# Splitting the first loads over two queues and shortening the run of filler products at the start of an AdaLN-FFN kernel

## The chip, the cores and the metric

One Trainium2 chip, one core of it. The metric is the device time of one execution in microseconds, median of several runs. TensorE (PE) does the matrix products, VectorE (DVE), ScalarE (ACT) and GpSimd (POOL) the elementwise work, and SyncE (SP) and ACT issue the DMAs that this text speaks of.

## The reference, cut to what matters

`x` is 64 x 64 x 512 in f32 (batch, row, feature) and `cond_1024` is 64 x 256. The first part of the computation is the one that the change touches:

```python
q_emb = relu(cond @ W3 + b3)                 # 64 x 512, "the condition"
v_sum = sum(v, axis=1, keepdims=True)        # over the 64 rows of a batch
x = (n * v + v_sum) * q_emb[:, None, :]      # "modulation", n = 64
y = relu(x @ W2 + b2)
```

The second part is an FFN on `y`: a base product with `W_base`, a shared low-rank product, six low-rank experts that are weighted by the two largest of six softmax gates, and their sum with the input.

## The kernel before

The features lie on the 128 partitions (512 = 4 chunks `c`), the 4096 rows along the free axis, in 4 blocks `k` of 1024 rows (16 batches of 64). Block 0 is done by `first_mixed`, blocks 1 to 3 by `first_inner`, and behind each comes the FFN. From the second half of block 0 on, the products use schemes with seven instead of eight partial products, whose operand sums DVE makes (`t2`, `inner_t`, `s`). The order on each engine is the order in which the program issues the instructions.

**The start.** SP issues the loads one after the other:

- `head_sb`, 196 KB: the condition, the two biases (136 columns of f32 in all, `NH0`) and the first quarter of W3 (256 columns);
- `xa` number 0, 128 KB: the first 4 batches of chunk 0; then `w2` chunk 0, 256 KB; `xa` number 1, the next 4 batches; `w3`, 384 KB, the other three quarters of W3; then `x0` and `w2` for the other chunks, in turn; the FFN's weights; and block 1 of `x`.

The DMAs of SP and ACT use eight completion semaphores in turn, so that a load is issued only when the one eight places ahead of it has landed.

On ACT a one-column activation (line 108) comes first, and with it the load of the activation table. On PE, `first_mixed` begins with `idle(8)`: eight bf16 products of a constant tile of ones, 128 x 512, whose output is not used. Then comes `embed([0], ...)`, the condition's product for the first 128 features: four matmuls (an f32 product is two matmuls here), which read `head_sb`, and an ACT Relu into `q_sb`. Then `idle(2)`. Then for each chunk `c`:

- `modulate_group` on DVE: the batch sums (line 245), `n * v + v_sum` (line 255, two instructions) and the product with `q_sb` (line 259);
- the products `py` (line 409) with the four output blocks `f` of `w2` chunk `c`. Chunk 0 is done in two pieces of 4 batches, eight matmuls each, and behind the first piece comes `embed(range(1, NC))`, twelve matmuls that need `w3`;
- `modulate_scalar` for the other eight batches of the chunk before: sums and two small products on DVE, then eight ACT instructions (line 267).

When the four chunks are done, DVE makes the sums `t`, `inner_t` and `s` (lines 141 to 154 and 280 to 283), of which the product at line 181 that follows is the first reader.

Of the kernel before, what the change touches and what calls it, by code (L numbers as in the profile page):

```python
# [16 lines left out]
P = 128  # L17
# [10 lines left out]
DH = D // 2  # L28
# [10 lines left out]
def adaln_ffn(ctx: ExitStack, tc: tile.TileContext, xa, x0, x1, head, w3, w2, wb, a, bcat, bb, br, outT):  # L39
# [8 lines left out]
    nc = tc.nc  # L48
# [12 lines left out]
    def temps(name):  # L61

        return {n: tmp.tile([P, KH, TB], F32, tag=n, name=f"{n}_{name}") for n in pair_tags}

    def load_x(k):
        xs[k] = xpool.tile([P, NC, 2, TB], F32, tag="x", name=f"x_{k}")
        for c in CHUNKS:
            nc.sync.dma_start(xs[k][:, c].rearrange("p h t -> p (h t)"), x1[k, c])
# [18 lines left out]
    NH0 = NQ * B + 2 * NC  # L87
    head_sb = const.tile([P, NH0 + NQ * P], F32, tag="head_sb", name="head_sb")
# [4 lines left out]
    w2_sb = const.tile([P, NC, D], F32, tag="w2_sb", name="w2_sb")  # L93
# [7 lines left out]
    def load_xa(n):  # L101
        nc.sync.dma_start(xs[0][:, 0, ts(n, TB // 2)], xa[n])

    def load_w2(c):
        nc.sync.dma_start(w2_sb[:, c, :], w2[ts(c, P), :])

    nc.sync.dma_start(head_sb, head)
    nc.scalar.activation(scratch, ones[:, :1], AF.Relu)
    load_xa(0)
    load_w2(0)  # L110
    load_xa(1)
    nc.sync.dma_start(w3_sb, w3)
    for c in range(1, NC):
# [75 lines left out]
    def idle(n):  # L189
        p = ps_p.tile([P, TB], F32, tag="pp", name="idle")  # L190
        for _ in range(n):
            nc.tensor.matmul(p, ones[:, :P], ones, start=True, stop=True)

    def embed(fs, name):
        pq = ps_h.tile([P, len(fs), B], F32, tag="ph", name=name)
        for n, f in enumerate(fs):
            for c in range(NQ):
                nc.tensor.matmul(
                    pq[:, n], w3_of[f][:, c], cond_sb[:, c, :], start=(c == 0), stop=(c == NQ - 1)
                )  # L200
        for n, f in enumerate(fs):
            nc.scalar.activation(q_sb[:, f, :], pq[:, n], AF.Relu, bias=b3_sb[:, f : f + 1])
# [44 lines left out]
    def modulate_group(v, vsum, c, lo, hi):  # L247

        nb = hi - lo
        batch_sums(vsum, c, lo, hi)  # L250
        xc = batches_of(c, lo, hi)
        vc = v[:, c, :, lo * NH : hi * NH].rearrange("p h (b n) -> p h b n", n=NH)
        sc = vsum[:, c, lo:hi]
        for h in range(2):
            nc.vector.scalar_tensor_tensor(
                vc[:, h], xc[:, h], float(N), sc.unsqueeze(2).to_broadcast([P, nb, NH]), ALU.mult, ALU.add
            )
        q = q_sb[:, c, lo:hi].unsqueeze(1).unsqueeze(3).to_broadcast([P, 2, nb, NH])
        nc.vector.tensor_tensor(vc, vc, q, ALU.mult)

    def modulate_scalar(v, vsum, nq, c, lo, hi):

        batch_sums(vsum, c, lo, hi)
        nc.vector.tensor_scalar(nq[:, c, lo:hi], q_sb[:, c, lo:hi], float(N), None, ALU.mult)
        nc.vector.tensor_tensor(vsum[:, c, lo:hi], vsum[:, c, lo:hi], q_sb[:, c, lo:hi], ALU.mult)  # L265
        for b in range(lo, hi):
            nc.scalar.activation(  # L267
                v[:, c, :, ts(b, NH)], batches_of(c, b, b + 1)[:, :, 0], AF.Identity,
                bias=vsum[:, c, b : b + 1], scale=nq[:, c, b : b + 1],
            )  # L270

    def row_sums(a, name, cols=slice(0, TB)):

        all_s = mid.tile([P, 4, KH, TB], F32, tag=name, name=name)
        s = [all_s[:, i, :, cols] for i in range(4)]
        a11, a12, a21, a22 = a[:, :KH, 0, cols], a[:, KH:, 0, cols], a[:, :KH, 1, cols], a[:, KH:, 1, cols]

        def steps(c=slice(0, KH), fourth=nc.vector):
            return [
                lambda: nc.vector.tensor_tensor(s[0][:, c], a21[:, c], a22[:, c], ALU.add),  # L280
                lambda: nc.vector.tensor_tensor(s[1][:, c], s[0][:, c], a11[:, c], ALU.subtract),
                lambda: nc.vector.tensor_tensor(s[2][:, c], a11[:, c], a21[:, c], ALU.subtract),
                lambda: fourth.tensor_tensor(s[3][:, c], a12[:, c], s[1][:, c], ALU.subtract),
            ]

        return {1: a11, 2: a12, 3: s[3], 4: a22, 5: s[0], 6: s[1], 7: s[2], "sums": all_s}, steps
# [6 lines left out]
    def fill(n):  # L293
        for _ in range(min(n, len(behind))):
            for step in behind.pop(0):
                step()
# [100 lines left out]
    def first_mixed(y):  # L397

        vs[0] = v = xpool.tile([P, NC, 2, TB], F32, tag="x", name="v_0")
        vsum = small.tile([P, NC, BB], F32, tag="vsum", name="vsum_0")
        nq = small.tile([P, NC, BB], F32, tag="nq", name="nq_0")
        half, cols = BB // 2, BB // 2 * NH
        other = slice(cols, TB)
        s, s_steps = row_sums(v, "s", other)

        def part(p, c, f, lo, hi):
            nc.tensor.matmul(  # L409
                p[:, :, lo * NH : hi * NH], w2_sb[:, c, ts(f, P)], v[:, c, :, lo * NH : hi * NH],  # L410
                start=(c == 0 and lo == 0), stop=(c == NC - 1), skip_group_check=True,
            )

        def without_sums(c):
            for j in range(KH):
                nc.tensor.matmul(
                    px[:, j], w2_sb[:, c, ts(j, P)], v[:, c, 0, other],
                    start=(c == 0 and j == 0), stop=(c % KH == KH - 1),
                    skip_group_check=True,
                )  # L420

        idle(8)
        embed([0], "pq0")
        idle(2)
        p0 = [ps_p.tile([P, 2, cols], F32, tag="pp", name=f"py_{f}") for f in range(NC)]

        px = ps_p.tile([P, KH, cols], F32, tag="pp", name="yx_0")
        p1 = mid.tile([P, 4, 1, R2], F32, tag="inner_s1", name="p1_0").rearrange("p n o t -> p (n o t)")
        p1 = p1[:, : KH * cols].rearrange("p (j t) -> p j t", j=KH)
        for c in range(NC):  # L430
            pieces = ((0, half // 2), (half // 2, half)) if c == 0 else ((0, half),)
            for lo, hi in pieces:
                modulate_group(v, vsum, c, lo, hi)
                for f in range(NC):
                    part(p0[f], c, f, lo, hi)
                if c == 0 and lo == 0:
                    embed(range(1, NC), "pq")
            if c > 0:
                modulate_scalar(v, vsum, nq, c - 1, half, BB)
            if c == KH:  # L440
                for n in range(KH):
                    without_sums(n)
        nc.scalar.copy(p1, px)
        modulate_scalar(v, vsum, nq, NC - 1, half, BB)
        for f in range(NC):
            nc.scalar.activation(y[:, f, :, :cols], p0[f], AF.Relu, bias=b2_sb[:, f : f + 1])
        for c in range(KH, NC):
            without_sums(c)
        load_x(2)
        for step in t2_steps + inner_steps[:4] + s_steps():  # L450
            step()
        prepare(1, tb_steps + inner_steps[4:])
        fill(1)
        pairs = temps(0)
        for j in range(KH):
            relu(y, j, 0, px[:, j], other)
        banks = [ps_p.tile([P, KH, cols], F32, tag="pp", name=f"y{n}_0") for n in "ywz"]
        for j in range(KH):
            f1, f2 = j, KH + j
            temp = lambda n: pairs[n][:, j, :cols]  # L460
            py, pw, pz = (p[:, j] for p in banks)
            u, r, r1, r2 = temp("u"), temp("u22"), temp("u21"), temp("u12")
            product(py, 6, j, t2, s, start=j == 0)
            nc.vector.tensor_tensor(u, py, p1[:, j], ALU.add)
            product(pw, 5, j, t2, s, start=j == 0)
            nc.vector.tensor_tensor(r, pw, u, ALU.add)
            product(pz, 7, j, t2, s, start=j == 0)
            nc.vector.tensor_tensor(r, pz, r, ALU.add)  # L468
            relu(y, f2, 1, r, other)
            fill(1)  # L470
            product(pw, 3, j, t2, s, start=False)
            nc.vector.tensor_tensor(r2, pw, u, ALU.add)
            relu(y, f2, 0, r2, other)
            fill(1)
            product(pz, 4, j, t2, s, start=False)
            nc.vector.tensor_tensor(r1, pz, u, ALU.add)
            relu(y, f1, 1, r1, other)
            fill(1)
# [921 lines left out]
```

## Time and profile before

| | |
|---|---|
| median of 3 runs | 253.53 us (253.40 to 253.58) |
| the profiled execution | 253.81 us, span 252.0 us |
| PE busy | 246.8 us, 98% of the span |
| DVE, ACT, POOL busy | 203.8, 158.0, 126.2 us |
| DMA | 33.82 MB, mean 134 GB/s |

The span runs from the first to the last profiled instruction of the program; 1.81 us of the profiled execution's time lie outside it. Times in the profile are us from the start of the span. In a row of the timeline stand the start, the time from the first start to the last end, engine, line, operation, output<-inputs, shapes, the number of instructions, and in brackets how long the engine had been idle and what released it. Names are given without their numbers: `w_sb` stands for `w2_sb` and `w3_sb`, `pq` for both of the condition's products. A matmul's printed duration is longer than its share of PE, since matmuls overlap; the distance between starts is what one costs.

### The profile page before, as it was taken

The page shows a single profiled execution, that of the slowest core. Times are in us where ns is not written, and L with a number is a line of the kernel's source. Part 1 is how long each engine was busy: PE and PEld are TensorE (multiplying, and loading weights), DVE is VectorE, ACT ScalarE, POOL GpSimd, SP SyncE. Part 2 cuts the span into 40 slices and gives each one's busy share as a digit, 9 for nine tenths or more (in the row PEclk, how much of TensorE's full clock was granted, in tenths as well). Part 3 has the DMA queues.
Part 4 walks back from the last instruction along what each step waited for, and adds up shares of the span by engine and source line. Part 5 has one row for each costly group of instructions (what it writes and reads, how often), then busy time and mean ns, then how long its engine had stood idle before and what let it go on. Part 6 is the DMA issues. An engine that isn't in the chain of part 4 may idle for free.

```text
span 252.0 us, 3678 instructions
## 1 busy us (share of the span) xinstructions
PE 246.8 (98%) x1134; PEld 189.4 (75%) x1134; DVE 203.8 (81%) x407; ACT 158.0 (63%) x436; POOL 126.2 (50%) x150
## 2 busy tenths in 40 slices
PE   8999999999999999999999999999999999999993
PEld 3846897454468889857888889947888889966783
DVE  2899998879996988999995778999992576797472
ACT  2299588579018889797638889796826428252310
POOL 1000000009707579059469968339659894059850
PEclk9999999999999999999999999999999999999999
DMA  6997818000431024835459922306259852500054
GB/s 181 370 350 274 330 28 307 0 3 16 151 125 42 3 86 138 336 147 216 61 80 195 156 94 101 127 25 250 28 79 197 138 133 97 166 1 0 9 194 134
DMA packets 17482, 33.82 MB, mean 134 GB/s; under 512 B 1605, under 2 KB 3781, under 8 KB 17462
## 3 DMA queue, kind: packets, MB, share of 16 engines
q1 hardware_dynamic: 13910, 27.09, 30.3%
q0 software_dynamic: 3264, 6.29, 15.9%
q10 hardware_dynamic: 288, 0.20, 0.3%
q8 instruction: 9, 0.15, 0.2%
q14 instruction: 11, 0.09, 0.1%
HBM read 19.94 MB, written 14.68 MB: 137 GB/s over the span
## 4 chain that ended last, share of the span: by engine, by line
PE 96%; DMA 2%; DVE 0%; SPq 0%; issue 0%
PE ia L502 14%; PE ph L1337 11%; PE ib L502 11%; PE ha L987 10%; PE hb L987 8%; PE oz L181 7%; PE py L409 6%; PE oy L181 6%; PE ja L987 4%; PE jb L987 3%; PE ox L181 3%; PE ow L181 3%; DMA w_sb<-in_w_dram 2%; PE yw L181 1%; PE pt L649 1%; PE yz L181 1%
## 5 line engine op out<-in xcount | busy, mean ns | idle before, releaser
L229 ACT ACTIVATE x<-x,vsum,nq 128x64 f32<-128x64 f32 x176 | 63.3, 431 | 1.4 <-DVE vsum L221 1.4
L656 POOL TENSOR_TENSOR hwd<-hwT 113x512 f32<-113x512 f32 x4 | 5.1, 1271 | 55.4 <-ACT hwT L651 55.4
L1337 PEld LDWEIGHTS ph<-a_sb,y 128*128 128x128 f32 x256 | 30.7, 192 | 0.8
L1337 PE MATMUL ph<-a_sb,y 128*128 128x118 f32 x256 | 30.7, 275 | 0.0
L493 DVE TENSOR_TENSOR u<-ib,u 128x256 f32<-128x256 f32 x42 | 16.4, 418 | 11.9 <-PE ib L502 11.8
L493 DVE TENSOR_TENSOR u<-ia,u 128x256 f32<-128x256 f32 (+1 forms) x36 | 16.1, 462 | 7.1 <-ACT u L540 5.8
L508 ACT COPY ib<-ia 128x256 f32<-128x256 f32 x21 | 7.6, 361 | 17.2 <-PE ia L502 17.2
L395 ACT ACTIVATE y<-u,head_sb 128x256 f32<-128x256 f32 (+1 forms) x30 | 15.8, 583 | 3.7 <-DVE u L468 3.0
L502 PE MATMUL ib<-inner_s,inner_t 128*128 128x256 f32 x60 | 17.4, 379 | 0.0
L219 DVE TENSOR_REDUCE vsum<-x 128x8 f32<-128x512 f32 x24 | 15.5, 676 | 0.0
L181 PE MATMUL oz<-sy,tb 128*128 128x512 f32 x32 | 15.0, 592 | 0.0
L409 PE MATMUL py<-v,w_sb 128*128 128x512 f32 (+1 forms) x40 | 14.4, 510 | 0.6 <-DMA w_sb<-in_w_dram 0.6
L181 PE MATMUL oy<-sy,tb 128*128 128x512 f32 x32 | 14.7, 597 | 0.0
L511 ACT COPY ib<-ib 128x256 f32<-128x256 f32 x21 | 7.6, 360 | 9.0 <-PE ib L502 8.6
L502 PEld LDWEIGHTS ib<-inner_s,inner_t 128*128 128x128 f32 x60 | 11.4, 190 | 1.6
L409 PEld LDWEIGHTS py<-v,w_sb 128*128 128x128 f32 x40 | 7.4, 190 | 6.7 <-issue 4.8
L344 POOL TENSOR_TENSOR sy<-sy 128x256 f32<-128x256 f32 x4 | 3.8, 952 | 17.2 <-PE oy L181 17.2
L267 ACT ACTIVATE v<-x,vsum,nq 128x64 f32<-128x64 f32 x32 | 11.0, 429 | 1.7 <-DVE vsum L265 1.7
L744 POOL DMA_DIRECT2D out_dram<-y x8 | 10.8, 1688 | 0.7 <-ACT ib L508 0.7
L181 PEld LDWEIGHTS oy<-sy,tb 128*128 128x128 f32 x32 | 5.8, 190 | 6.8 <-issue 6.2
L502 PE MATMUL ia<-s,t 128*128 128x256 f32 x36 | 10.2, 379 | 0.0
L181 PEld LDWEIGHTS oz<-sy,tb 128*128 128x128 f32 x32 | 5.8, 190 | 5.8 <-issue 5.3
(321 smaller groups left out, 679.9 us busy)
## 6 DMA issues: line engine op xcount, KB each, us to landing
xu<-in_x_dram SPq DMA_DIRECT2D x14, 512.0 KB, 4.4
out_dram<-xu SPq DMA_DIRECT2D x25, 256.0 KB, 2.2
x<-in_x_dram SPq DMA_DIRECT2D x12, 512.0 KB, 7.5
out_dram<-y POOLq DMA_DIRECT2D x8, 512.0 KB, 9.4
out_dram<-inner_tb POOLq DMA_DIRECT2D x4, 512.0 KB, 5.9
x<-in_x_dram SPq DMA_DIRECT2D x7, 256.0 KB, 5.7
w_sb<-in_w_dram SPq DMA_DIRECT2D x4, 256.0 KB, 5.5
wb_sb<-in_wb_dram SPq DMA_DIRECT2D x4, 256.0 KB, 5.0
```

The costliest lines, as they stand in the source:

```text
L181: nc.tensor.matmul(ps, w[i][:, c, ts(j, P)], s[i][:, c, :], start=start and c == 0, stop=c == KH - 1, skip_group_check=True,)
L219: nc.vector.tensor_reduce(vsum[:, c, bs], xc, AX.XY, ALU.add)
L229: nc.scalar.activation(x, x, AF.Identity, bias=bias, scale=scale)
L267: nc.scalar.activation(v[:, c, :, ts(b, NH)], batches_of(c, b, b + 1)[:, :, 0], AF.Identity, bias=vsum[:, c, b : b + 1], scale=nq[:, c, b ...
L395: nc.scalar.activation(y[:, f, h, cols], src, AF.Relu, bias=b2_sb[:, f : f + 1])
L409: nc.tensor.matmul(p[:, :, lo * NH : hi * NH], w2_sb[:, c, ts(f, P)], v[:, c, :, lo * NH : hi * NH], start=(c == 0 and lo == 0), stop=(c = ...
L493: add = lambda o, a, b: nc.vector.tensor_tensor(o, a, b, ALU.add)
L502: nc.tensor.matmul(bank[b, t][:, cols], t_side(o, n), s_side(o, n), start=n == 1, stop=True, skip_group_check=True,)
L508: nc.scalar.copy(bank["b", t][:, lo], bank["a", t][:, lo])
L744: nc.gpsimd.dma_start(outT[k, f : f + KH, h].rearrange("f p t -> p f t"), parts[o], accum_op=ALU.add)
L987: nc.tensor.matmul(p, w, s, start=start, stop=True, skip_group_check=True)
L1337: nc.tensor.matmul(ph[:, h * NS + s, :HC], y[:, c, h, ts(s, P)], a_sb[:, c, :], start=(c == 0), stop=(c == NC - 1),)
```

## The change

The first loads are issued in another order and on two queues. `xa` number 0 is first on SP. `head_sb` comes in two parts: the 256 columns of W3 (128 KB) on ACT's queue, the 136 columns of condition and biases (68 KB) on SP, behind `xa`. `w2` chunk 0 comes in two halves of 256 columns (128 KB each): the half for the output blocks 0 and 1 on ACT, the half for the blocks 2 and 3 on SP. ACT issues its two loads ahead of its first activation. From `xa` number 1 on the order on SP is what it was. On PE two of the eight products of ones ahead of the condition's product go, and one of the two behind it.

```diff
-    nc.sync.dma_start(head_sb, head)
+
+    half_w2 = [slice(n * DH, (n + 1) * DH) for n in range(2)]
+    load_xa(0)
+    nc.scalar.dma_start(head_sb[:, NH0:], head[:, NH0:])
+    nc.sync.dma_start(head_sb[:, :NH0], head[:, :NH0])
+    nc.scalar.dma_start(w2_sb[:, 0, half_w2[0]], w2[:P, half_w2[0]])
     nc.scalar.activation(scratch, ones[:, :1], AF.Relu)
-    load_xa(0)
-    load_w2(0)
+    nc.sync.dma_start(w2_sb[:, 0, half_w2[1]], w2[:P, half_w2[1]])
     load_xa(1)
     nc.sync.dma_start(w3_sb, w3)
...
-        idle(8)
+        idle(6)
         embed([0], "pq0")
-        idle(2)
+        idle(1)
```

## The prediction

> **What bounds the kernel now.** I read the page first, then the chain of waits of the first 35 us, the timeline of the first 14 us, the windows of the start, and the timeline around 25 us. The page:
>
> ```profile
> PE 246.8 (98%) x1134; PEld 189.4 (75%) x1134; DVE 203.8 (81%) x407; ACT 158.0 (63%) x436; POOL 126.2 (50%) x150
> ...
> PE 96%; DMA 2%; DVE 0%; SPq 0%; issue 0%
> ```
>
> PE is busy for nearly the whole span and is nearly the whole chain, so what the start loses or wins is carried to the end. The only DMA on the chain is at the start, as the chain of waits from 0 to 35 us has it (start, us, what):
>
> ```profile
> 1.63 4.78 DMA w_sb<-in_w_dram
> 6.41 0.14 issue
> 6.55 1.97 PE py L409 x8
> 8.51 1.28 PE pq L198 x12
> 9.80 8.65 PE py L409 x24
> ```
>
> The first real product waits for `w2` chunk 0, issued at 1.63 and landed at 6.41. The timeline of the first 14 us shows what stands beside it:
>
> ```profile
> 0.74 1.28 ACT L108 ACT_TABLE_LOAD   x1 [0.74 <-PEq L1386]
> ...
> 0.78 3.57 PE L192 MATMUL idle<-const-bfloat16-1.0 128*128 128x512 bf16 x8 [0.78 <-PEq L1386]
> ...
> 3.56 0.42 DVE L245 TENSOR_REDUCE vsum<-x 128x4 f32<-128x256 f32 x1 [3.56 <-DMA x<-in_xa_dram]
> ...
> 4.14 0.95 PE L198 MATMUL pq<-head_sb 128*128 128x64 f32 x4
> ...
> 5.48 0.42 DVE L259 TENSOR_TENSOR v<-v,q_sb 128x256 f32<-128x256 f32 x1 [0.97 <-ACT q_sb L202]
> ...
> 7.72 0.33 SPq L105 DMA_DIRECT2D w_sb<-in_w_dram  x1
> ...
> 8.35 1.45 PE L198 MATMUL pq<-head_sb,w_sb 128*128 128x64 f32 x12
> 8.39 1.00 SPq L99 DMA_DIRECT2D x<-in_x_dram  x2
> 8.39 0.69 DVE L245 TENSOR_REDUCE vsum<-x 128x8 f32<-128x512 f32 x1 [0.21 <-DMA x<-in_x_dram]
> ...
> 10.18 0.69 DVE L259 TENSOR_TENSOR v<-v,q_sb 128x512 f32<-128x512 f32 x1 [0.30 <-ACT q_sb L202]
> ```
>
> Three bounds lie close behind one another: `w2` at 6.41, against `v` at 5.90 (5.48 + 0.42); `w3`, seen landing at 7.72, when SP may issue the load eight places behind it, for the twelve matmuls at 8.35; and `x0` of chunk 1, landing at 8.39, for the DVE work that ends in line 259 at 10.18. The timeline around 25 us shows why the last one counts:
>
> ```profile
> 24.39 0.69 DVE L281 TENSOR_TENSOR s<-s,v 128x512 f32<-128x512 f32 x1
> ...
> 25.23 1.10 PE L181 MATMUL yy<-s,t 128*128 128x256 f32 x4
> ```
>
> The sum `s` is done at 25.08 and the product that reads it starts at 25.23. From 10.18 to there DVE has no pause over 0.1 us, so PE and DVE arrive together: PE can start no earlier there than DVE lets it.
>
> **The change, part by part.** The sum is made against the profiled execution, 253.81 us (span 252.0 and 1.81 outside it); the median of the runs is 0.28 lower.
>
> *Products of ones.* Eight of them start at 0.78 and the condition's product follows at 4.14: 0.42 each. Six end at 3.30, so this removes 0.84 ahead of the condition. The one taken behind it frees 0.43 between 4.89 and 5.75, where PE would wait for `v` anyway: worth nothing by itself. What both cost if the clock needs them is the second rival.
>
> *Condition.* Both parts of `head_sb` must have landed. In the trace the second load on SP, issued at 1.18, released DVE at 3.56 with 324 KB read until then. In the new order the second load on SP, again at 1.18, is the second part of `head_sb`, and with the two loads ahead of it it makes the same 324 KB; ACT's share starts at 0.74. So 3.55 is nearest. Bounds: 3.2, what the first load takes now (0.74 + 2.5 from issue to landing), and 5.96, if it is held as `w2` is (1.18 + 4.78). With 0.14 from landing to first product (6.41 to 6.55) the condition's product starts at 3.69 instead of 4.14, 0.45 earlier. Then `q_sb` and line 259 follow at their distances: line 259 at 5.03, its end at 5.45, a product possible at 5.6. The batch sums and line 255 are under cover: DVE idled 0.97 ahead of line 259, and `xa` is now the first load.
>
> *`w2` chunk 0.* Output blocks 0 and 1 need the first half alone. ACT issues it behind 0.38 for `head_sb` (its two late issues, lines 1258 and 1268, took 0.38 and 0.36), at 1.15, 0.48 before SP does now. Bounds of its landing: 3.05, by ACT's 128 KB store of line 1258, which landed 1.9 after issue, and 5.93, by the 4.78 of `w2` itself. Half of the bytes, read at the same place, I put in the middle, 4.5: then `v` is the last to come, and the first product starts at 5.6 instead of 6.55, a gain of 0.95 (at the late bound 6.07, a gain of 0.48). The second half has the issue slot that all of `w2` has now, so 6.41 at the latest; it is needed four matmuls later, at 5.6 + 4 x 0.22 = 6.46. ACT's table load and first activation (1.28 and 0.20) move back by 0.76; they would end near 3.0, and the Relu queued behind them needs ACT only at 4.69.
>
> *What comes after.* SP still issues three loads ahead of `xa` number 1, so this one and `w3` keep their slots at 2.11 and 2.58 and have the same 708 KB and 1,092 KB up to and with them. Two more loads use up semaphores, and `w2` chunk 1 must now wait for `xa` number 0; that landed long before its slot at 3.53. If nothing lands sooner, `w3` at 7.72 allows the twelve matmuls at 7.86 instead of 8.35 (gain 0.49), and `x0` allows line 259 only the 0.30 that it waited for `q_sb` at 10.18. With d as the time by which the loads behind `w2` land sooner, the gain at 25 us is the least of 0.95, 0.49 + d and 0.30 + d. The windows (us, busy times, then granted clock, DMA share and GB/s) bound d:
>
> ```profile
> 0.78:2.43 1.65, 1.65 (x4) 0.56 (x5) 0.00 (x0) 1.44 (x2) 0.85 (x10) 1.00 0.36 82
> 2.43:5.84 3.41, 3.41 (x11) 1.69 (x9) 1.27 (x4) 0.31 (x1) 0.00 (x0) 1.00 0.91 250
> ...
> 9.25:12.70 3.45, 3.45 (x16) 2.53 (x16) 3.11 (x9) 1.66 (x6) 0.00 (x0) 1.00 1.06 401
> ```
>
> From 2.43 to 5.84 the DMAs moved 250 GB/s, later 401. The hole is worth 3.41 x 151/401 = 1.28 us; in it `w2` was slow, with 4.78 where the loads ahead of it took 2.4 to 2.5. So d is at most 1.28, if the second queue fills the hole. It is zero if the hole only moves with the same bytes, and below zero if two streams disturb each other. I take the time by which `w2` is first read sooner, 0.48. The least of the three is then 0.78, on the DVE side.
>
> [...]
>
> The sum: 253.81 - 0.78 = 253.03, less 0.28 for the median: 252.75 us.
>
> **The rivals.** *Hidden by the loads behind.* d lies between -0.3 and 0.2, and `x0` of chunk 1 holds DVE: a gain of 0 to 0.5, time 253.0 to 253.5, middle 253.25. For it: the bytes and issue slots up to `w3` are the same. Against it: the hole begins with `w2`, whose first read moves.
>
> *The clock stays low, and the kernel is slower.* The condition's first four matmuls take 0.95 and the twelve later ones 1.45, 0.24 against 0.12 each: PE runs at half speed at 4.9 and at full speed from 6.55. Something in between, at about 5.84, raised it, after PE had been busy in 3.3 of the 3.41 us ahead of it, while the stretch of that length before, with 1.65 busy (48%), had not done so. Now that stretch would hold 0.87 of ones, 1.18 of condition and one product of ones, and 0.24 of real products: 2.3, or 67%. Where between 48% and 97% it tips, no row shows; that decides. If it fails, products of 0.43 run from 5.6 to 9.02, two of the twelve go at the slow rate, and the rest at 0.11 end near 10.46 instead of 9.63: 0.83 slower, 254.35. The runs of before lie within 0.18, which speaks for a mark that is met with room, and so for less than 97%.
>
> [...]
>
> *The loads come later.* If ACT's table load went ahead of its issues, or the two streams hold each other up as `w2` is held now, `head_sb` and `w2` land about 0.8 later than they do now: near 254.3. Against it: the table load belongs to the activation, behind the two issues in program order, and ACT and SP issued at the same time at 248.5 with no more than 0.36 and 0.42.
>
> **How the numbers follow.** The gain 0.50; hidden 0.20; the clock 0.22; late loads 0.08. About 0.2%, 0.5 us, is what a measurement of this kernel can tell from no change, so faster 0.50, same 0.20, slower 0.30. The range goes from 252.2, a gain of 1.3 with `head_sb` at its early bound (first product 5.26) and d near 1.0, to 254.4, which takes in the price of the clock.
>
> **What would show it.** Right: the first product `py` between 5.4 and 5.8, released by `v` and not by `w2`; the twelve condition matmuls near 7.5; line 259 of chunk 1 near 9.4; no PE pause at the sums near 24.5. The hidden case: a PE pause ahead of the twelve or near 25. The clock: first `py` matmuls 0.43 apart past 5.9. Late loads: `py` behind `w_sb` at 6.5 or more. The prediction is wrong if `w3` or `x0` of chunk 1 lands later than 7.7 and 8.4.

## The result and the profile after

The changed kernel takes 254.47 us (median of 6 runs, 254.13 to 254.76) where the kernel before took 253.42 in the runs beside it (252.79 to 253.58): a ratio of 1.0044, 95% interval 1.0033 to 1.0054. It is 1.05 us slower. The forecast was 252.75 with a range to 254.4, so the time lies just outside the range, on the side of the second rival, the clock, which had been given 0.22 and a price of 254.35. The profiled execution took 254.76, with a span of 253.0 (before: 253.81 and 252.0).

Line numbers of the changed kernel are four higher from `first_mixed` on (the condition's matmuls 202, `py` 413, line 259 is now 263, 181 is 185). The page has the same work and the same engine as the bound:

```profile
PE 247.5 (98%) x1131; PEld 190.0 (75%) x1131; DVE 203.9 (81%) x407; ACT 158.0 (62%) x436; POOL 127.2 (50%) x150
...
PE 96%; DMA 1%; DVE 1%; SPq 0%; issue 0%; ACT 0%
```

The chain of waits from 0 to 35 us starts elsewhere, though:

```profile
1.19 2.84 DMA head_sb<-in_head_dram
4.03 0.14 issue
4.17 1.10 PE pq L202 x4
5.27 0.02 issue
5.29 0.32 ACT q_sb L206
5.62 0.02 issue
5.64 0.43 DVE v L263
6.08 0.04 issue
6.12 3.76 PE py L413 x8
9.88 1.28 PE pq L202 x12
```

`w2` is off the chain, as intended; the condition's second part, landing at 4.03, has taken its place, and by way of `q_sb` and `v` the first product starts at 6.12, 0.43 sooner than before. Then the same eight matmuls take 3.76 instead of 1.97. The timeline of the first 14 us shows both pauses of PE and what comes of them:

```profile
0.78 2.72 PE L196 MATMUL idle<-const-bfloat16-1.0 128*128 128x512 bf16 x6 [0.78 <-PEq L1390]
...
4.17 1.09 PE L202 MATMUL pq<-head_sb 128*128 128x64 f32 x4 [0.66 <-DMA head_sb<-in_head_dram]
...
5.05 0.63 PE L196 MATMUL idle<-const-bfloat16-1.0 128*128 128x512 bf16 x1
...
6.12 3.76 PE L413 MATMUL py<-v,w_sb 128*128 128x256 f32 x8 [0.44 <-DVE v L263]
...
8.70 0.69 DVE L249 TENSOR_REDUCE vsum<-x 128x8 f32<-128x512 f32 x1 [1.14 <-DMA x<-in_x_dram]
...
9.69 1.47 PE L202 MATMUL pq<-head_sb,w_sb 128*128 128x64 f32 x12
...
11.55 0.69 DVE L263 TENSOR_TENSOR v<-v,q_sb 128x512 f32<-128x512 f32 x1 [1.37 <-ACT q_sb L206]
```

From 6.12 to 9.69 the eight `py` matmuls start 0.43 apart (0.59 behind the first; 0.22 apart in before) and the twelve after them 0.11: PE ran at half speed until about 9.7. The trace's record of the clock has its first stretch at full speed from 9.73; in the trace of before it is from 5.84. (The clock column of the windows says 1.00 for the time ahead of that too, since the record has no entry there.) That is 3.61 us at half speed, an estimated 1.80 lost, less the 0.43 by which `py` starts sooner: 1.37, which is the distance of line 259 of chunk 1 (11.55 against 10.18). PE is 1.36 late from there up to 200 matmuls before its end and 1.20 late at its last one; the span ends 1.0 later. The last 0.36 are time that the profiled execution of before lost by itself: e3's trace, an experiment below, gains the same 0.16 on it between those matmuls and 0.21 behind the last one.

### The profile page after: what moved, and what is told of

Read it like the earlier page. It is cut to its first block, busy times and chain, and to the rows that moved or that the text cites. A ratio compares the mean times of both kernels' runs of the same rounds, so it can differ in the third digit from the quotient of the medians.

```text
span 253.0 us, 3675 instructions
## 1 busy us (share of the span) xinstructions
PE 247.5 (98%) x1131; PEld 190.0 (75%) x1131; DVE 203.9 (81%) x407; ACT 158.0 (62%) x436; POOL 127.2 (50%) x150
## 4 chain that ended last, share of the span: by engine, by line
PE 96%; DMA 1%; DVE 1%; SPq 0%; issue 0%; ACT 0%
PE ia L506 14%; PE ph L1341 11%; PE ib L506 11%; PE ha L991 10%; PE hb L991 8%; PE oz L185 7%; PE py L413 6%; PE oy L185 5%; PE ja L991 4%; PE jb L991 3%; PE ox L185 3%; PE ow L185 3%; PE yw L185 1%; PE pt L653 1%; PE yz L185 1%; PE yx L420 1%
## 5 line engine op out<-in xcount | busy, mean ns | idle before, releaser
L413 PE MATMUL py<-v,w_sb 128*128 128x512 f32 (+1 forms) x40 | 16.2, 563 | 0.4 <-DVE v L263 0.4
L413 PEld LDWEIGHTS py<-v,w_sb 128*128 128x128 f32 x40 | 8.5, 218 | 6.6 <-issue 4.8
L748 POOL DMA_DIRECT2D out_dram<-inner_tb x4 | 4.9, 1235 | 10.6 <-DVE inner_s L348 5.5
```

Of the source, the lines that this page charges most:

```text
L413: nc.tensor.matmul(p[:, :, lo * NH : hi * NH], w2_sb[:, c, ts(f, P)], v[:, c, :, lo * NH : hi * NH], start=(c == 0 and lo == 0), stop=(c = ...
L748: nc.gpsimd.dma_start(outT[k, f : f + KH, h].rearrange("f p t -> p f t"), parts[o], accum_op=ALU.add)
```

## The experiments

The theories were: C, the clock, with late full speed because PE pauses between its filler products; L, the loads, with `w3` and `x0` 0.3 later and two streams in each other's way; and, for the gain that was forecast, B, that `x0` of chunk 1 and the DVE work behind it hold it back whatever the start does. Each kernel was run beside the kernel before on the same chip (medians of before: 253.44 beside e1 to e4, 253.45 beside e5 to e8, 253.53 beside e9 and e10, 253.44 beside e11 and e12). The ratios are not those of the medians given; where executions fall into two groups the two can point different ways, as in e10.

**The two halves of the change, apart.** The first kernel is the change with `idle(8)` and `idle(2)`, the second the kernel before with

```diff
-        idle(8)
+        idle(6)
         embed([0], "pq0")
-        idle(2)
+        idle(1)
```

> The new loads with the old eight and two products of ones. Theory C (the clock: the fewer products of ones leave PE idle so long that full speed comes one stretch of 3.41 us later): PE stays busy from 0.78 to about 5.9 as in the kernel before, the products py run 0.22 apart from their first one at about 6.1, the twelve condition matmuls start near 8.2 on w3, and the time is that of the kernel before, 253.2 to 253.6. Theory L (the loads: w3 and x0 of chunk 1, 0.3 later than before, and two streams that disturb each other, cost the time): 254.0 to 254.5 as with the whole change.

> The old loads with six and one products of ones. Theory C: the condition comes about 0.7 sooner, but PE then idles for two us until w2 lands at 6.4, the products py start at half speed, 0.43 apart, and the time is 254.2 to 254.9. Theory L: the loads are the old ones, so 253.2 to 253.6.

The loads alone: 253.37 (12 runs, 252.62 to 253.69), ratio 0.9986 (0.9964 to 1.0008). The counts alone: 253.69, ratio 1.0017 (0.9986 to 1.0048), but in two groups: seven executions from 253.15 to 253.70 ("in time" from here on) and five from 254.83 to 256.51 ("late"). Its profiled execution was one of the late ones (255.15), with full speed from 10.08. So the loss is in the counts, as C has it, and not in the loads. C's expectation for the second was only half right: more than half of the executions are in time, and its slowest, 256.51, is later than one missed stretch explains and has no trace.

**Which pause.** The new loads with three products behind the condition, and with either removal alone:

```diff
         idle(8)   # e3: 8 and 3;  e4: 6 and 2;  e5: 8 and 1
         embed([0], "pq0")
         idle(3)
```

> The new loads with eight products of ones ahead and three behind, so that PE has no pause from 0.78 until v is there at 6.1. Theory C: full speed before py in every execution, 253.1 to 253.5, and a spread of the runs under 0.3. If the gain that was forecast for the loads is there once the clock is, 252.9 or less. Theory L: 254.0 to 254.5.

> The new loads with six products of ones ahead and two behind: the pause ahead of the condition's product (3.3 to 4.2) stays, the one behind it shrinks from 0.64 to about 0.2. Theory C, if the share of a 3.41 us stretch in which PE is busy decides: the stretch up to py goes from 56% to some 70%; between e1 and the whole change, 253.4 to 254.5, with a spread over 0.4. Theory L: 254.0 to 254.5 with the spread of before.

> The new loads with eight products of ones ahead and one behind: the pause ahead of the condition's product is closed, the one between it and py (about 5.5 to 6.0) stays. Theory C: a stretch of 3.41 us that holds only this pause is busy for 84% or more; the stretches seen so far raised the clock at 97% and more and did not at 72% and less, so most executions are in time: median 253.2 to 253.7, and a late one now and then near 255. If it is the number of products of ones and not the pause that counts, nine instead of ten of them: between e1 and the whole change, 253.8 or more.

Without any pause (e3): 253.32, 252.95 to 253.88, ratio 0.9989 (0.9969 to 1.001), so no late group, but a spread of 0.9 where under 0.3 was expected. With the pause ahead of the condition (e4): median 254.1, three executions from 252.59 to 253.24 and nine from 253.94 to 254.89. With the pause behind it alone (e5): 253.47, nine of eleven from 252.91 to 253.51 and two at 254.6. It is the two products ahead that cost most of it.

**The whole change in an execution that is in time.** To part the clock from all else, the whole change was run with `w3` in two parts (that edit follows with e7):

> The whole change, six and one, with w3 in two parts. Theory C: the late clock costs here what it costs in the change, so 1.0 to 1.5 over e7: 253.6 to 254.1, most executions late. If the late part of the change came from the loads and not from the clock, 252.6 as e7.

The executions fall into two groups again: five from 252.39 to 253.02, seven from 254.21 to 255.26 (median 254.24, ratio 0.9994, 0.9966 to 1.0023). One program, one set of loads, and 1.8 us between the groups. All six runs of the change itself were late; as e10 has the same products of ones, a longer series of it would probably hold some in time as well, which was not run. The profiled one belongs to the first group (252.39), and beside the late one of e4 it shows how little decides. First the PE rows of the timeline of e4, then those of e10 (lines two higher again):

```profile
0.78 2.72 PE L196 MATMUL idle<-const-bfloat16-1.0 128*128 128x512 bf16 x6 [0.78 <-PEq L1390]
...
4.07 1.08 PE L202 MATMUL pq<-head_sb 128*128 128x64 f32 x4 [0.57 <-DMA head_sb<-in_head_dram]
...
4.95 1.06 PE L196 MATMUL idle<-const-bfloat16-1.0 128*128 128x512 bf16 x2
...
6.02 3.78 PE L413 MATMUL py<-v,w_sb 128*128 128x256 f32 x8
```

```profile
0.78 2.72 PE L198 MATMUL idle<-const-bfloat16-1.0 128*128 128x512 bf16 x6 [0.78 <-PEq L1392]
...
4.15 0.63 PE L204 MATMUL pq<-head_sb 128*128 128x64 f32 x4 [0.65 <-DMA head_sb<-in_head_dram]
...
5.64 1.99 PE L415 MATMUL py<-v,w_sb 128*128 128x256 f32 x8 [0.65 <-DVE v L265]
```

e4 has the smaller pauses and the slow `py` (3.78); e10 has the larger ones, and yet its condition matmuls (0.63 instead of 1.08) and `py` (1.99) run at full speed. What differs is where the stretches of 3.41 us lie. Their length is measured: in all fourteen profiles the clock record's first time at full speed lasts 242.35, 245.76 or 249.17 us (245.76 in before, 242.35 in the change), which lie 3.41 apart and are 71, 72 and 73 times 3.413. The clock record has full speed from 3.95 in e10 and from 9.67 in e4, and in the fourteen profiles it begins at 5.84, 9.73, 5.54, 10.08, 6.54, 9.67, 4.43, 3.60, 6.05, 6.04, 5.85, 3.95, 4.51 and 5.24: the stretches stand anew against the kernel in each execution. The three starts past 9.6 are those of the change, e2 and e4, whose profiled executions were all late. Counting back from there in steps of 3.41, taking it that a stretch ends where full speed begins, and with a matmul counted from its start to the next one's (to 0.2 before its printed end ahead of a pause), the stretches that raised the clock were busy for these shares, and those that did not:

| | share of PE busy |
|---|---|
| raised it, lowest four | 74% (e10), 83% (e6), 92% (e8), 97% (before, e9) |
| did not, highest four | 72% (e2), 71% (e4), 69% (e3), 62% (after) |

In this counting the fourteen profiles part between 72% and 74%. The margin is thin, and it needs the counting by starts: by printed durations, which overlap, e4's stretch has 83% and failed, e10's 80% and passed. With six and one, the stretch that the pauses fall in has 56% in the profile of the change; with the pauses closed, every stretch that begins at -0.1 or later would hold 74% or more, so that full speed would come by 6.7 at the latest, an estimate from the table (e1 and e3 have it from 5.54 and 6.54), and none of the 24 executions of e1 and e3 is over 253.9. A stretch missed costs about half of 3.41, 1.7 us, an estimate from the half speed of `py` above; e10's two groups are some 1.8 apart.

**The late ones of the kernel before.** In the runs beside these experiments, 8 of its 107 executions were over 254.2 (up to 255.77).

> The kernel before with four instead of two products of ones behind the condition, so that PE has no pause from 0.78 to 6.5, when w2 lands. Theory C: the rare executions of before at 254.8 to 255.8 are those whose stretch fell on the pause from 5.75 to 6.55, so here none is over 254.3, with the same median, 253.2 to 253.6. If these rare executions have another cause, about one in ten stays there.

None of the 11 is over 253.82; the median is 253.47, ratio 1.0001 (0.9992 to 1.001). At 8 in 107, none in 11 would be found four times in ten by chance, so the cause of these executions stays open.

**Where the gain of the loads went.** In e3 the clock is in time and the products start 0.38 sooner than before, yet its ratio of 0.9989 can't be told from no change. Its timeline, at the start and around 25 us:

```profile
6.17 2.08 PE L413 MATMUL py<-v,w_sb 128*128 128x256 f32 x8
...
8.53 0.69 DVE L249 TENSOR_REDUCE vsum<-x 128x8 f32<-128x512 f32 x1 [0.23 <-DMA x<-in_x_dram]
...
10.11 0.69 DVE L263 TENSOR_TENSOR v<-v,q_sb 128x512 f32<-128x512 f32 x1
```

```profile
23.18 1.89 PE L420 MATMUL yx<-v,w_sb 128*128 128x256 f32 x8
...
24.31 0.69 DVE L285 TENSOR_TENSOR s<-s,v 128x512 f32<-128x512 f32 x1
...
25.12 0.73 PEld L185 LDWEIGHTS yy<-s,t 128*128 128x128 f32 x4 [0.45 <-PE yx L420]
25.15 1.10 PE L185 MATMUL yy<-s,t 128*128 128x256 f32 x4
```

`x0` releases DVE no sooner (8.53 against 8.39), line 259 starts 0.07 sooner, the sum of line 281 (285 here) 0.08, and so does the product at 25.15. PE itself is 0.26 sooner at the products `yx` ahead of it (23.18); their row in the timeline of before:

```profile
23.44 1.89 PE L416 MATMUL yx<-v,w_sb 128*128 128x256 f32 x8
```

So 0.18 of PE's gain is lost there, waiting for DVE. Two kernels test this. The first starts `py` sooner still, with the condition's loads ahead of the rows:

```diff
-    load_xa(0)
     nc.scalar.dma_start(head_sb[:, NH0:], head[:, NH0:])
     nc.sync.dma_start(head_sb[:, :NH0], head[:, :NH0])
+    load_xa(0)
```

> The new loads with the condition's loads first and the rows behind them on SP, seven and two products of ones. The condition's product starts near 3.75 instead of 4.15 and py near 5.5 instead of 6.0. Theory B: w3, as late as ever at 7.8 to 8.0, then lets PE pause ahead of the twelve matmuls, and the time is that of e3, 253.1 to 253.5. If the start of py is what counts, as the forecast had it, 252.7 to 252.9.

It takes 253.67, ratio 1.0011 (1.0001 to 1.0021), a little more than B expected. The timeline of its profiled execution, with 254.37 one of the two slowest of eleven:

```profile
5.59 2.32 PE L413 MATMUL py<-v,w_sb 128*128 128x256 f32 x8
...
8.95 1.52 PE L202 MATMUL pq<-head_sb,w_sb 128*128 128x64 f32 x12 [1.04 <-DMA w_sb<-in_w_dram]
...
9.54 0.69 DVE L249 TENSOR_REDUCE vsum<-x 128x8 f32<-128x512 f32 x1 [1.03 <-DMA x<-in_x_dram]
```

`py` starts at 5.59, a whole 0.96 sooner than before, and PE then stands for 1.04 until `w3` lands. The second kernel gives `x0` of chunk 1 fewer bytes to wait for:

```diff
-    nc.sync.dma_start(w3_sb, w3)
+    nc.sync.dma_start(w3_sb[:, 0], w3[:, 0])
     for c in range(1, NC):
         load_x0(c, 0)
+        if c == 1:
+            nc.sync.dma_start(w3_sb[:, 1:], w3[:, 1:])
...
-                if c == 0 and lo == 0:
-                    embed(range(1, NC), "pq")
+                if c == 0:
+                    embed([1] if lo == 0 else range(2, NC), f"pq_{lo}")
```

> The new loads with eight and three, and w3 in two parts: the quarter for features 128 to 255 in its old place, the other two behind x0 of chunk 1, and their condition matmuls behind the second piece of py instead of the first. Theory B (with the clock in time, x0 of chunk 1 and the DVE work behind it hold the gain of the loads back): x0 has 256 KB less ahead of it and lands near 7.9 instead of 8.5, line 259 of chunk 1 starts near 9.8 instead of 10.1, and the time is 0.2 to 0.4 under e3: 252.9 to 253.15. If DVE does not hold it back, e3's 253.3.

252.63 (6 runs, 252.22 to 252.79), ratio 0.9964 (0.995 to 0.9978), a larger gain than expected. The rows that carry it:

```profile
7.65 0.68 DVE L251 TENSOR_REDUCE vsum<-x 128x8 f32<-128x512 f32 x1
7.87 0.55 PE L204 MATMUL pq<-head_sb,w_sb 128*128 128x64 f32 x4
...
9.23 0.69 DVE L265 TENSOR_TENSOR v<-v,q_sb 128x512 f32<-128x512 f32 x1
...
23.73 0.69 DVE L287 TENSOR_TENSOR s<-s,v 128x512 f32<-128x512 f32 x1
...
24.69 1.03 PE L187 MATMUL yy<-s,t 128*128 128x256 f32 x4
```

`x0` no longer releases DVE at all (it had landed at 7.32; DVE came from other work at 7.65), line 259 (265 here) starts at 9.23 instead of 10.11, and the kernel gains 0.7 us over e3. The sum of line 281 (287 here) starts 0.58 sooner than in e3, the product that reads `s` 0.46. Between the two traces PE is 0.22 sooner ahead of these products, with full speed from 6.05 instead of 6.54, and 0.57 sooner behind them; this 0.35, gained where PE waits for DVE's sums, is B. B is shown in that, and the 0.22 is the clock's, by chance. The same edit on the kernel before tells what of it needs the new loads:

> The kernel before, loads and eight and two as they were, with w3 in two parts as in e7. If e7's gain is that of w3 and x0 alone: 252.6 to 252.9 here too. If it takes the new loads as well (py at 6.55 instead of 6.1 then sets the pace): 253.0 to 253.3.

252.9 (12 runs), ratio 0.9972 (0.9955 to 0.999): at the upper end of the first expectation. Most of the gain is that of `w3` and `x0`; what the new loads add, 0.1 to 0.3 us between e9 and e7, lies inside the intervals. The last two, on one chip:

> e7 with the condition's loads ahead of the rows on SP, and seven and three products of ones. With w3 and x0 no longer holding the gain back, the earlier condition (3.75 instead of 4.15) should now count: py near 5.6, 252.2 to 252.5, against 252.6 for e7. If x0 of chunk 1 and DVE still set the pace, 252.6 to 252.9.

> e7 once more, on the chip of e11 and of another six or more runs: 252.5 to 252.8, no execution over 253.2, faster than before by 0.25% to 0.45%.

e11: 252.59 (5 runs), ratio 0.9966 (0.9954 to 0.9979), at the lower edge of the second expectation: the earlier start is worth nothing that can be told here (0.13 between the medians of e11 and e12). e12: 252.72 (11 runs, 252.24 to 253.32), ratio 0.9968 (0.9959 to 0.9977). Its slowest execution was the profiled one, 0.1 over what was expected of any. e7 is the fastest version found together with e11, 0.3% under the kernel before.

## Why the prediction was wrong

The rivals were the right ones, and two of them hold at once: the clock, and the loads behind. The likeliest case was the wrong choice. The step that made the kernel slower is the clock's: the sum left full speed at 5.84, where it was, and it came at 9.73. Two terms of the sum were wrong besides, the condition's landing and d; with them put right its gain would have been 0.30 or less instead of 0.78 (0.30 + d, with d nothing or below).

- *Condition* (3.69 forecast, 4.17 measured). The 324 KB were to land as they do on one queue, at 3.55. On two queues, with the first half of `w2` read beside them, the last of the condition landed at 4.03, and at 3.77 to 3.95 in e1, e3, e4 and e5; that it is this company that delays it was not tried. The matmuls came no sooner than before, and the two products of ones taken away ahead of them became a pause of PE.
- *First product* (5.6 forecast, 6.12 measured). `v` came last, as forecast, and the first half of `w2` landed at 4.35, where 4.5 was taken. The 0.5 is that of the condition, passed on. The 6.55 that it was to beat is one execution's, too: with the old loads `py` started at 6.55, 6.26, 6.00 and 5.96 in before, e6, e2 and e9, with `w2` landing at 6.41, 6.13, 5.86 and 5.68.
- *The clock* (0.22 given, nothing in the sum). The price of 0.83 was worked out for `py` at 5.6; with it at 6.12 and full speed from 9.73 the same working gives the 1.37 between the profiles. That 254.35 lies so near the measured 254.47 is luck in part, since the 0.36 that the profile of before lost by itself sets off most of this difference. The step that failed is the weighing: a share of 67% was found to lie between one that fails at 48% and one that passes at 97%, and the narrow runs of before were taken to say that the mark, which no run had shown then, is met with room. Three runs are few for that: of 107 executions of before eight were over 254.2. And the parting between 72% and 74%, as the fourteen profiles show it, leaves room for 97% and none for 67%, nor for the 56% that it was. That the clock goes by stretches of 3.41 us, as the weighing has it, no row of the prediction shows; the lengths of the times at full speed, 3.41 apart in the fourteen profiles, do. Besides, the stretches were taken to lie where they lie in the profile of before, while each execution has its own: the same kernel is in time once and late the next time, and a price must be given for each place of them.
- *What comes after* (d, 0.48 forecast). `x0` of chunk 1 landed at 8.68 (8.26 to 8.73 in e1, e3, e4, e5) against 8.37, 9.33 and 8.10 with the old loads (before, e2, e6): d is nothing, or below it. The signs named for a wrong forecast came, `w3` at 8.00 and `x0` at 8.68. The hole in the DMA's work was taken to belong to `w2` and to move with it. It does not: in the changed kernel both halves of `w2` had landed by 5.04, and `w3` landed 1.87 after `xa` number 1 (0.95 in before); in e2, where `w2` landed at 5.86, `x0` came 1.66 after `w3` (0.67 in before). So the hidden case, 253.25, is about what the new loads give with the clock in time: e1 has 253.37, e3 253.32.
- *Late loads* (0.08 given). The half of this rival that put ACT's table load ahead of its two issues fell: the issues took 0.41 and 0.45 at 0.74 and 1.18, beside SP's, and the table load came behind at 1.66, hidden as forecast. The other half, two streams that hold each other up, agrees with the condition's landing (all of `head_sb` by 4.03, against 3.24 before), though the cause was not tried, but not with the price: e1 has 253.37, not 254.3.

## What to carry to other kernels

Filler products ahead of the first real work are not free time to be cut to the arrival of data: e10, with two pauses of 0.65 us among them, has its executions in two groups 1.8 us apart, while e1 and e3, with a pause of 0.17 and with none, have none of 24 over 253.9; full speed began anywhere from 3.60 to 10.08 us, so look at the spread of many executions and not at one trace. A load that stands last in the chain is worth moving only up to the next one: list when each following load lands and which engine it releases before putting a gain on the first. Here 256 KB moved behind the load that DVE waits for gave 0.3%, and an earlier first product gave nothing that could be told from the spread.

## What the runs showed of the hardware

- In the fourteen profiles, PE busy counted by starts, the stretch of 3.41 us just ahead of full speed was always busy for 74% or more, and those that full speed did not follow for 72% or less; full speed has no fixed distance from the kernel's start (3.60 to 6.54 where it was in time, 9.67 to 10.08 where it was late).
- Among the first loads some landed late, and not the same ones in each profile: `w2` in before (4.78 from issue, where the loads ahead of it took 2.4 to 2.5), its second half in e3 (4.9, against 3.4 in the change), `x0` in e2 (1.66 after `w3`), `w3` in the change (1.87 after `xa`). What holds them is open; it was not tried.
- SP and ACT issued loads side by side at 0.74 in the change, in 0.39 and 0.41 us; SP alone took 0.38 to 0.43 for the first seven in before.
